# The end of a graph-network kernel: the last rows before the next-to-last batch's closing stages, and the last batch interleaved with it

## The chip, the cores and the metric

The kernel runs on one core of one Trainium2 chip, in one launch. The metric is the device time in microseconds, the median of 3 runs. The core has five engines that run side by side and meet at semaphores: TensorE (PE in the profile; PEld is its weight load), VectorE (DVE), ScalarE (ACT), GpSimd (POOL) and SyncE (SP, which here only issues transfers).

## What is computed

One message-passing layer over 6250 nodes of 128 features and 100000 edges, sorted by destination, with a residual sum and two layer norms. Cut to what matters:

```python
msg_in = concat([x[src], x[dst], edge_attr])           # (100000, 128 + 128 + 4)
h = silu(msg_in @ mW1 + mb1)
messages = h @ mW2 + mb2
aggregated = segment_sum(messages, dst, num_segments=6250)
u = silu(concat([x, aggregated]) @ uW1 + ub1)
updated = u @ uW2 + ub2
y = layer_norm(x + updated, ln_g, ln_b)
out = layernorm(x + y)
```

All of it is float32.

## The kernel before, in words

**Tables.** First, x @ mW1's source part is written to DRAM as `tab_a`, and the destination part as `tab_b`. x is also kept transposed in SBUF (`xT`).

**Edges.** The 100000 edges are cut into 98 groups (`NG`) of 1024, each of 8 tiles of 128 edges; the last group, 97, has 6 tiles. For each group, GpSimd gathers the source rows of `tab_a` by an indirect DMA for each tile (`fetch`, L277) into a tile `ga`, of which a ring of 6 exists. TensorE makes the destination part (`products`, L623) in a PSUM tile `pre` (two buffers). VectorE adds the two (`hidden`, L640), ScalarE takes the Silu (L641) into `h`. TensorE then multiplies h by a one-hot matrix of destinations (`sums`, L652, 16 instructions for 8 tiles), and VectorE adds the result to the running table `acc` and, once in four groups, the degrees to `deg` (`add`, L665 and L670). One pass of the loop at L680 does one group and issues the gathers of the group two ahead.

**Node batches.** What comes after the sum, for each node, is done in batches of 4 tiles of 128 nodes, in `node_batch` (L466). The next-to-last batch has 3 tiles (from tile 44) and the last one 2 (117 nodes by 2). `node_batch` is a generator: each `next` issues one stage, and `advance` issues one stage of every running batch. A batch starts when the groups that reach its nodes have been added. The stages of an ordinary batch are:

1. load of `xs` (x, L495), copies of its part of acc and deg (L500, L501)
2. matmuls into y: u1x by xT (L510), mb2u by degrees (L511), w2u by sums (L515)
3. Silu into uT (L518)
4. bias and u2 matmuls (L521, L530)
5. y + xs and its moments (L532, L483, L484), xs + bias of the norm (L535)
6. square root for the standard deviation (L489)
7. reciprocal, norm into z, moments of z (L539 to L548)
8. square root (L489)
9. reciprocal and shift on VectorE (L552, L554)
10. scale and shift on ScalarE (Identity, L560)
11. write to the output (L564)

The last batch (`final=True`) reads `acc` and `deg` in place, makes two versions of x by two VectorE adds at its second stage (L507, L508), and has one more `yield` between L511 and L515. Its tiles come from the ring of `ga`, and its y is a buffer of `pre`. Before its load stands a VectorE memset (L494), as its tile isn't filled to 128 partitions.

**Order.** The order of all instructions on the engines is the order in which the code issues them (a manual schedule). The next-to-last batch starts in the pass of group 95 with four stages; the pass of group 96 issues four more, ending with stage 8. After the loop come, in this order: the last batch's load; a one-element Silu (`primed`, L748) that brings ScalarE's Silu table back; add(96); the last batch's second stage; the last group's rows in two pieces (`piece`, L731: add L732, Silu L733, sums L652); add(97); two stages of the last batch; and then the rest of both batches, stage by stage in turn.

Of the kernel before, what the change touches and what calls it, by code (L numbers as in the profile page):

```python
# [8 lines left out]
F32 = mybir.dt.float32  # L9
# [3 lines left out]
OP = mybir.AluOpType  # L13
# [5 lines left out]
P = 128  # L19
# [5 lines left out]
def kernel(  # L25
# [40 lines left out]
    nc = tc.nc  # L66
    N, H = x.shape
# [4 lines left out]
    G = 8  # L72
    GE = G * P
    NG = -(-E // GE)
# [11 lines left out]
    BT = 4  # L86
# [16 lines left out]
    batches = [(i0, n, (i0 + n) * P * E // (N * GE) + 1) for i0, n in groups(NT - LAST, BT)]  # L103
# [315 lines left out]
    def rows_ps():  # L419
        return ps.tile([P, G, P], F32, name="pre")  # L420
# [45 lines left out]
    def node_batch(i0, n, work, new, y, final=False):  # L466

        cols = slice(i0 * P, (i0 + n) * P)
        m = (min((i0 + n) * P, N) - i0 * P) // n
        assert m * n == min((i0 + n) * P, N) - i0 * P  # L470

        def rows_of(t):

            return t[i0 * P : i0 * P + m * n].rearrange("(p j) f -> p j f", j=n)

        def flat(t):
            return t[:, :n].rearrange("p i f -> p (i f)")

        def moments(v):
            mv = work.tile([P, BT, 2], F32, name="mv", bufs=2)  # L480
            for i in range(n):
                st = work.tile([P, 6], F32, name="st", bufs=2)
                nc.vector.bn_stats(st, v[:, i, :])  # L483
                nc.vector.bn_aggr(mv[:, i, :], st)  # L484
            return mv

        def std(mv):
            r = work.tile([P, BT], F32, name="r", bufs=2)
            nc.scalar.activation(r[:, :n], mv[:, :n, 1], AF.Sqrt, bias=eps)  # L489
            return r  # L490

        xs = new("xs")
        if m < P:
            nc.vector.memset(xs[m // 32 * 32 :, :n], 0.0)  # L494
        nc.sync.dma_start(xs[:m, :n], rows_of(x))  # L495
        sums, counts = acc[:, cols], deg[:, cols]
        if not final:

            acc_b, deg_b = new("acc_b"), new("deg_b", DR)
            nc.scalar.copy(flat(acc_b), sums)  # L500
            nc.scalar.copy(flat(deg_b), counts)  # L501
            sums, counts = flat(acc_b), flat(deg_b)
        yield
        xb = xs
        if final:
            xb = new("xb")
            nc.vector.tensor_add(xb[:, :n], xs[:, :n], b_b[:, None, :].to_broadcast([P, n, H]))  # L507
            nc.vector.tensor_add(xs[:, :n], xs[:, :n], ub2_b[:, None, :].to_broadcast([P, n, H]))  # L508
        y = y()
        nc.tensor.matmul(flat(y), u1x, xT[:, cols], start=True, stop=False)  # L510
        nc.tensor.matmul(flat(y), mb2u, counts, start=False, stop=False)  # L511
        if final:

            yield
        nc.tensor.matmul(flat(y), w2u, sums, start=False, stop=True)  # L515
        yield
        uT = new("uT")
        nc.scalar.activation(flat(uT), flat(y), AF.Silu, bias=ub1_col)  # L518
        yield
        if not final:  # L520
            nc.tensor.matmul(  # L521
                y[:, :n],
                ones[0:1, :],
                ub2_row[:, None, :].to_broadcast([1, n, H]),
                start=True,
                stop=False,
            )
        by_p = flat(uT).rearrange("k (p j) -> k p j", j=n)
        for i in range(n):
            nc.tensor.matmul(y[:, i, :], by_p[:, :, i], u2, start=final, stop=final or i == n - 1)  # L530
        yield
        nc.vector.tensor_add(y[:, :n], y[:, :n], xs[:, :n])  # L532
        mv = moments(y)
        if not final:
            nc.vector.tensor_add(xs[:, :n], xs[:, :n], b_b[:, None, :].to_broadcast([P, n, H]))  # L535
        yield
        r = std(mv)
        yield
        nc.vector.reciprocal(r[:, :n], r[:, :n])  # L539
        z = new("z")  # L540
        for i in range(n):
            nc.vector.scalar_tensor_tensor(
                y[:, i, :], y[:, i, :], mv[:, i, 0:1], g_b, op0=OP.subtract, op1=OP.mult
            )
            nc.vector.scalar_tensor_tensor(
                z[:, i, :], y[:, i, :], r[:, i : i + 1], xb[:, i, :], op0=OP.mult, op1=OP.add
            )
        mz = moments(z)  # L548
        yield
        rz = std(mz)  # L550
        yield
        nc.vector.reciprocal(rz[:, :n], rz[:, :n])  # L552
        shift = work.tile([P, BT], F32, name="shift", bufs=2)
        nc.vector.scalar_tensor_tensor(  # L554
            shift[:, :n], mz[:, :n, 0], -1.0, rz[:, :n], op0=OP.mult, op1=OP.mult
        )
        yield
        o = z
        for i in range(n):
            nc.scalar.activation(  # L560
                o[:, i, :], z[:, i, :], AF.Identity, bias=shift[:, i : i + 1], scale=rz[:, i : i + 1]
            )
        yield
        (nc.scalar if final else nc.sync).dma_start(rows_of(out), o[:m, :n])  # L564

    def node_tiles(pool, y):
        return pool, lambda name, p=P: pool.tile([p, BT, H], F32, name=name), y
# [1 line left out]
    def advance(running):  # L569

        for b in list(running):
            if next(b, running) is running:
                running.remove(b)
# [70 lines left out]
    def degrees(g):  # L644
        pt = ps.tile([P, 2 * W], F32, name="pt")
        if g % DQ == 0:
            nc.tensor.transpose(pt[:DR, W:], deg_q[g // DQ % 2], ident[:W, :W])  # L647
        return pt
# [14 lines left out]
    def add(g, pt):  # L663
        at = acc[:, bass.ds(bases[g], W)]
        nc.vector.tensor_add(at, at, pt[:, :W])  # L665
        if g % DQ == 0:
            for k in range(min(DQ, NG - g)):
                row = slice(32 * k, 32 * k + 1)
                at = deg[row, bass.ds(bases[g + k], W)]
                nc.vector.tensor_add(at, at, pt[row, W:])  # L670
# [9 lines left out]
    for g in range(NG):  # L680
        if g == 1:
            load_weights()
        if g == 2:
            running.append(destination_checks(node_y()))
        if g == 8:
            running.append(fuse_weights())
        for c in range(1, NC):
            if g == max(1, c * EC // GE - 10):
                attributes(c)
            if g == max(1, c * EC // GE - 10) + 1:  # L690
                attribute_rows(c)
        if g + LEAD < NG:
            load(g + LEAD)
        last = g >= NG - 1
        if not last:
            h[g] = hidden(g)
        if g + 2 < NG:
            pre[g + 2] = products(g + 2)
        if g + MADE < NG:
            node_matrix(g + MADE)  # L700
        if g + 1 < NG:
            oh[g + 1] = edge_matrix(g + 1)
        if g - 2 in pt:
            add(g - 2, pt.pop(g - 2))
        if last:
            break
        pt[g] = by_nodes(g, h.pop(g), oh.pop(g))
        if CLOSE <= g + 2 < NG:
            fetch(g + 2, begun[g + 2], summing[g])
        elif g == 0:  # L710
            fetch(7, ended[1], begun[2])
        elif g == 1:
            fetch(8, begun[3], summing[1])
        elif g % 2:
            fetch(g // 2 + 8, ended[g + 1], begun[g + 2] if g == CLOSE - 3 else ended[g + 2])
        if g >= NG - 3:
            add(g - 1, pt.pop(g - 1))
        for i0, n, first in batches[:-1]:
            if g == (first if first >= NG - 3 else first + 1):
                running.append(node_batch(i0, n, *node_tiles(nodes, node_y)))  # L720
        for _ in range(4 if g >= NG - 3 else 2 if g >= NG - 6 else 1):
            advance(running)

    g = NG - 1
    n = tiles_of(g)
    ga, pg, oh_g, h_g = rows.pop(g), pre.pop(g), oh.pop(g), hbuf[g % NH]
    s = work.tile([P, G, H], F32, name="s")
    primed = consts.tile([1, 1], F32, name="primed")
    before = running.pop()

    def piece(lo, hi):  # L731
        nc.vector.tensor_add(s[:, lo:hi], ga[:, lo:hi], pg[:, lo:hi])  # L732
        nc.scalar.activation(h_g[:, lo:hi], s[:, lo:hi], AF.Silu)  # L733
        sums(g, pt[g], h_g, oh_g, lo, hi)

    final = node_batch(
        *batches[-1][:2],
        nodes,

        lambda name, p=P: gath.tile([P, G, H], F32, name="ga")[:p, :BT],  # L740
        lambda: rows_ps()[:, :BT],
        final=True,
    )
    while running:
        advance(running)
    next(final)

    nc.scalar.activation(primed, ones[0:1, 0:1], AF.Silu)  # L748
    add(g - 1, pt.pop(g - 1))
    pt[g] = degrees(g)  # L750
    next(final)
    piece(0, n - 2)
    piece(n - 2, n)
    add(g, pt.pop(g))
    for _ in range(2):
        next(final)
    running = [before, final]
    while running:
        advance(running)
# [157 lines left out]
```

## Time and profile before

| | us |
|---|---|
| median of 3 runs | 1012.25 (1011.08 to 1012.56) |
| the profiled execution | 1179.78 |
| its span, first to last instruction | 1177.7 |
| the last group's first row add (L732) starts at | 1159.17 |
| the last write (L564, from ScalarE's queue) is issued at | 1172.79 |

The profiled execution is longer than the runs that are timed. Times in views of the profile are counted from the span's start. The granted TensorE clock is 0.668 of full speed in the mean of the span. A chain of waits is read backwards from the last instruction: at each step it goes to what released the instruction, or to the one before it on the same engine, and so names what ended last.

### The profile page before, as it was taken

How to read it: one execution, taken by the hardware profiler on the slowest of the kernel's cores; microseconds unless marked ns; L12 is line 12 of the kernel's file. 1: busy time of each engine (PE TensorE's matmuls, PEld its weight loads, DVE VectorE, ACT ScalarE, POOL GpSimd, SP SyncE). 2: the span in 40 equal slices, each digit the busy share in tenths (PEclk: the TensorE clock that was granted, in tenths of full speed). 3: DMA queues.
4: the chain of work that ended last, by engine and by line, in shares of the span. 5: the costliest groups of instructions: out<-in, count | busy, mean ns of one | idle time of the engine just before them, and what ended most of it. 6: DMA issues, size and time to landing. Idle time of an engine off the chain costs nothing.

```text
span 1177.7 us, 11313 instructions
## 1 busy us (share of the span) xinstructions
PE 747.7 (63%) x3645; PEld 675.3 (57%) x3645; DVE 486.4 (41%) x1017; ACT 238.9 (20%) x297; POOL 743.2 (63%) x790
## 2 busy tenths in 40 slices
PE   5776896656756666567647666656566565656654
PEld 4575786555655656465646565555565464656533
DVE  4461654433532523532533353342343252353344
ACT  2211121220321311120221121121132131122132
POOL 6646666665666666666666666666666666656660
PEclk9877877676565666567566667666666667667665
DMA  8762232222222221222222213221222222212110
GB/s 198 203 156 71 75 85 65 67 82 61 74 66 73 67 72 52 79 72 73 55 72 76 58 57 81 65 81 56 71 74 66 71 74 63 65 55 69 47 59 20
DMA packets 70076, 89.01 MB, mean 76 GB/s; under 512 B 20703, under 2 KB 51694, under 8 KB 70010
## 3 DMA queue, kind: packets, MB, share of 16 engines
q0 software_dynamic: 25024, 51.30, 15.8%
q1 hardware_dynamic: 40408, 35.03, 10.3%
q10 hardware_dynamic: 4578, 1.89, 0.7%
q8 instruction: 31, 0.51, 0.2%
q14 instruction: 35, 0.29, 0.1%
HBM read 76.78 MB, written 11.38 MB: 75 GB/s over the span
## 4 chain that ended last, share of the span: by engine, by line
PE 35%; issue 32%; POOL 20%; DVE 2%; DMA 1%; another core or an unknown queue 1%; ACT 1%; DVEq 0%; POOLq 0%; SPq 0%; ACTq 0%
POOL ga L277 20%; PE pre L623 17%; PE pt L652 14%; PE pre L626 1%; PE y L530 1%; DMA ga<-tab_a,src_i 1%; PE y L521 1%; PE y L510 1%; PE y L511 0%; PE y L515 0%; DVE s L640 0%; DVE st L483 0%; DVE oh L609 0%; PE pt L647 0%
## 5 line engine op out<-in xcount | busy, mean ns | idle before, releaser
L277 POOL DMA_INDIRECT ga<-tab_a,src_i x742 | 703.7, 948 | 384.2 <-issue 187.1
L623 PE MATMUL pre<-mv,st 100*128 100x128 f32 x1564 | 345.1, 396 | 229.5 <-issue 199.5
L623 PEld LDWEIGHTS pre<-mv,st 100*128 100x128 f32 x1564 | 315.2, 301 | 248.4 <-issue 224.3
L652 PE MATMUL pt<-oh,h 128*128 128x96 f32 x1564 | 293.7, 348 | 147.6 <-issue 143.8
L652 PEld LDWEIGHTS pt<-oh,h 128*128 128x128 f32 x1564 | 279.9, 266 | 165.8 <-issue 162.3
L640 DVE TENSOR_TENSOR s<-ga,pre 128x1024 f32<-128x1024 f32 x92 | 112.2, 1220 | 502.6 <-DMA ga<-tab_a,src_i 419.8
L641 ACT ACTIVATE h<-s 128x1024 f32<-128x1024 f32 x92 | 97.1, 1056 | 671.5 <-issue 409.6
L596 DVE TENSOR_SCALAR_CACHE_REDUCE st<-near,p_next 96x1024 f32<-96x1024 uint8 x98 | 124.3, 1270 | 2.9 <-DMA near<-near_d 1.5
L609 DVE TENSOR_TENSOR oh<-w_row,rel 128x768 f32<-128x768 f32 x98 | 93.0, 949 | 42.5 <-remote 42.2
L277 POOL DMA_INDIRECT ga<-in_x_dram,src_i x32 | 30.7, 960 | 16.4 <-issue 8.8
L532 DVE TENSOR_TENSOR y<-y,xs 128x512 f32<-128x512 f32 (+1 forms) x12 | 8.3, 688 | 74.4 <-issue 70.7
L641 ACT ACT_TABLE_LOAD x23 | 29.5, 1283 | 24.2 <-PE pre L626 17.6
L489 ACT ACT_TABLE_LOAD x24 | 30.8, 1283 | 6.1 <-DVE st L483 5.7
L377 PE MATMUL wide<-w,xT 128*128 128x256 f32 x98 | 27.6, 441 | 3.5 <-DVE x_sb L380 3.5
L665 DVE TENSOR_TENSOR acc<-acc,pt 128x96 f32 x98 | 23.7, 242 | 12.5 <-PE pt L652 7.7
L530 PEld LDWEIGHTS y<-u,uT 128*128 128x128 f32 x94 | 22.7, 326 | 10.7 <-issue 10.7
L518 ACT ACTIVATE uT<-y,ub_col 128x512 f32<-128x512 f32 (+1 forms) x12 | 8.1, 678 | 96.5 <-remote 83.6
L377 PEld LDWEIGHTS wide<-w,xT 128*128 128x128 f32 x98 | 21.5, 227 | 8.3 <-DVE x_sb L380 4.3
L530 PE MATMUL y<-u,uT 128*128 128x128 f32 x94 | 25.4, 423 | 0.0
L670 DVE TENSOR_TENSOR deg<-deg,pt 1x96 f32 x98 | 24.4, 249 | 1.0
L626 PE MATMUL pre<-w,ga 128*128 128x128 f32 x80 | 19.4, 326 | 2.7 <-issue 2.6
L521 PE MATMUL y<-ub_row,ones 1*128 1x512 f32 (+1 forms) x24 | 15.5, 729 | 6.9 <-ACT uT L518 6.9
(118 smaller groups left out, 361.7 us busy)
## 6 DMA issues: line engine op xcount, KB each, us to landing
ga<-tab_a,src_i POOLq DMA_INDIRECT x742
near<-near_d SPq DMA_DIRECT2D x24, 384.0 KB
mv<-tab_b SPq DMA_DIRECT2D x98, 48.0 KB
tab_a<-t SPq DMA_DIRECT2D x6, 512.0 KB
tab_b<-x_sb SPq DMA_DIRECT2D x6, 512.0 KB
xs<-in_x_dram SPq DMA_DIRECT2D x11, 256.0 KB
out_dram<-z SPq DMA_DIRECT2D x11, 256.0 KB
st<-ea_d SPq DMA_DIRECT2D x98, 16.0 KB
```

Of the source, the lines that this page charges most:

```text
L277: ins = nc.gpsimd.indirect_dma_start(out=rows[g][:, i, :], out_offset=None, in_=x if g < RAW else tab_a[:, :], in_offset=bass.IndirectOffs ...
L377: ins = nc.tensor.matmul(pm[:, j], xT[:, cols], w1, start=True, stop=True)
L489: nc.scalar.activation(r[:, :n], mv[:, :n, 1], AF.Sqrt, bias=eps)
L521: nc.tensor.matmul(y[:, :n], ones[0:1, :], ub2_row[:, None, :].to_broadcast([1, n, H]), start=True, stop=False,)
L530: nc.tensor.matmul(y[:, i, :], by_p[:, :, i], u2, start=final, stop=final or i == n - 1)
L596: nc.vector.tensor_scalar(stbuf[g % NST][:W], near.pop(g), p_next, 0.0, op0=OP.is_equal, op1=OP.add, accum_out=deg_q[g // DQ % 2][:, g % D ...
L609: nc.vector.tensor_tensor(oh, w_row[:, None, :].to_broadcast([P, G, W]), rel[:, g, :, None].to_broadcast([P, G, W]), op=OP.is_equal,)
L623: ins = nc.tensor.matmul(pre[:, i, :], st[:, i, :], mv[g % NM], start=True, stop=g >= RAW)
L626: ins = nc.tensor.matmul(pre[:, i, :], rows[g][:, i, :], w1[:, 0, :], start=False, stop=True)
L640: nc.vector.tensor_add(s[:, :n], ga[:, :n], ps[:, :n])
L641: nc.scalar.activation(h[:, :n], s[:, :n], AF.Silu)
L652: ins = nc.tensor.matmul(pt[:, :W], h[:, i, :], oh[:, i, :], start=i == 0, stop=i == tiles_of(g) - 1)
```

## The change

It has four parts.

- In the pass of group 95 the last batch is created and its first stage issued (memset and load of x). In the pass of group 96 the next-to-last batch is not advanced at all (it was by four stages), and the last batch's second stage is issued: the two adds of x and the u1x matmul. The extra `yield` stands ahead of the mb2u matmul now, so this moves to the third stage.
- After the loop the last group's rows come first, in two pieces as before, and then add(96).
- Then come the remaining stages of both batches in an order written out by hand: two of the next-to-last batch, the one-element Silu, add(97), and then the two in turn.
- At the end of the last batch, the shift on VectorE and the two Identity passes on ScalarE give way to one subtract-and-multiply on VectorE for each tile (`tensor_scalar`), and the write follows from ScalarE's queue in the same stage.

```diff
@@ node_batch
         nc.tensor.matmul(flat(y), u1x, xT[:, cols], start=True, stop=False)
+        if final:
+
+            yield
         nc.tensor.matmul(flat(y), mb2u, counts, start=False, stop=False)
-        if final:
-
-            yield
         nc.tensor.matmul(flat(y), w2u, sums, start=False, stop=True)
...
         nc.vector.reciprocal(rz[:, :n], rz[:, :n])
+        if final:
+            for i in range(n):
+                nc.vector.tensor_scalar(
+                    z[:, i, :], z[:, i, :], mz[:, i, 0:1], rz[:, i : i + 1],
+                    op0=OP.subtract, op1=OP.mult,
+                )
+            nc.scalar.dma_start(rows_of(out), z[:m, :n])
+            return
...
-        (nc.scalar if final else nc.sync).dma_start(rows_of(out), o[:m, :n])
+        nc.sync.dma_start(rows_of(out), o[:m, :n])
@@ the loop over groups
-        for _ in range(4 if g >= NG - 3 else 2 if g >= NG - 6 else 1):
+        for _ in range(0 if g == NG - 2 else 4 if g == NG - 3 else 2 if g >= NG - 6 else 1):
             advance(running)
+        if g == NG - 3:
+            final = node_batch(
...
+                final=True,
+            )
+            next(final)
+        if g == NG - 2:
+            next(final)
@@ after the loop
-    before = running.pop()
-
-    def piece(lo, hi):
+    (before,) = running
+    pt[g] = degrees(g)
+    for lo, hi in ((0, n - 2), (n - 2, n)):
         nc.vector.tensor_add(s[:, lo:hi], ga[:, lo:hi], pg[:, lo:hi])
         nc.scalar.activation(h_g[:, lo:hi], s[:, lo:hi], AF.Silu)
         sums(g, pt[g], h_g, oh_g, lo, hi)
-
-    final = node_batch(
...
-    while running:
-        advance(running)
+    add(g - 1, pt.pop(g - 1))
+    next(before)
+    next(before)
+
+    nc.scalar.activation(primed, ones[0:1, 0:1], AF.Silu)
+    add(g, pt.pop(g))
     next(final)
-
-    nc.scalar.activation(primed, ones[0:1, 0:1], AF.Silu)
-    add(g - 1, pt.pop(g - 1))
-    pt[g] = degrees(g)
     next(final)
-    piece(0, n - 2)
-    piece(n - 2, n)
-    add(g, pt.pop(g))
-    for _ in range(2):
-        next(final)
+    next(before)
+    next(final)
+    next(before)
+    next(final)
+    next(final)
+    next(before)
+    next(final)
     running = [before, final]
     while running:
         advance(running)
```

More of the change, by code (lines that the diff above doesn't have):

```diff
@@ L510, in node_batch @@
         nc.tensor.matmul(flat(y), u1x, xT[:, cols], start=True, stop=False)
-        nc.tensor.matmul(flat(y), mb2u, counts, start=False, stop=False)
         if final:
             yield
+        nc.tensor.matmul(flat(y), mb2u, counts, start=False, stop=False)
         nc.tensor.matmul(flat(y), w2u, sums, start=False, stop=True)
@@ L720 @@
                 running.append(node_batch(i0, n, *node_tiles(nodes, node_y)))
-        for _ in range(4 if g >= NG - 3 else 2 if g >= NG - 6 else 1):
+        for _ in range(0 if g == NG - 2 else 4 if g == NG - 3 else 2 if g >= NG - 6 else 1):
             advance(running)
+        if g == NG - 3:
+            final = node_batch(
+                *batches[-1][:2],
+                nodes,
+                lambda name, p=P: gath.tile([P, G, H], F32, name="ga")[:p, :BT],
+                lambda: rows_ps()[:, :BT],
+                final=True,
[3 more added lines that the diff above has]
+            next(final)
     g = NG - 1
@@ L734, in piece @@
         sums(g, pt[g], h_g, oh_g, lo, hi)
-    final = node_batch(
[L737 to L743, printed above, removed]
-    while running:
-        advance(running)
+    add(g - 1, pt.pop(g - 1))
[3 more added lines that the diff above has]
+    add(g, pt.pop(g))
     next(final)
-    nc.scalar.activation(primed, ones[0:1, 0:1], AF.Silu)
-    add(g - 1, pt.pop(g - 1))
-    pt[g] = degrees(g)
     next(final)
-    piece(0, n - 2)
-    piece(n - 2, n)
-    add(g, pt.pop(g))
-    for _ in range(2):
-        next(final)
+    next(before)
[5 more added lines that the diff above has]
+    next(final)
     running = [before, final]
```

## The prediction

> **What bounds the kernel now.** I read the page first (busy shares, issues), then the table of waits, then the chain of waits over the last 33 us, then the timeline of the same stretch. The page says that no engine is full, and that GpSimd with its gathers is the most regular of them:
>
> ```profile
> PE 747.7 (63%) x3645; PEld 675.3 (57%) x3645; DVE 486.4 (41%) x1017; ACT 238.9 (20%) x297; POOL 743.2 (63%) x790
> L277 POOL DMA_INDIRECT ga<-tab_a,src_i x742 | 703.7, 948 | 384.2 <-issue 187.1
> ```
>
> and the table of waits says how the gathers wait:
>
> ```profile
> DVE s L640 <- DMA ga<-tab_a,src_i: 419.8, 65, 10.6
> POOL ga L277 <- remote: 141.4, 48, 3.6
> ```
>
> Until the last gather the loop follows GpSimd: a gather starts every 1.25 us, and VectorE waits 419.8 us in all for gathered rows. The 141.4 us of "remote" pauses have no releaser in the program. They are near the 167.5 us by which the profiled execution (1179.78) is longer than the median (1012.25), so I don't take them to be part of the unprofiled time. The change touches nothing before group 95, so all it can move lies after about 1136 us. There the chain of waits reads (start, length, what):
>
> ```profile
> 1149.82 0.58 DVE y L532
> ...
> 1154.46 0.21 DVE st L483
> ...
> 1155.78 0.28 DVE ga L494
> 1156.08 2.08 DMA ga<-in_x_dram
> 1158.16 0.03 issue
> 1158.21 0.04 issue
> 1158.25 0.44 DVE ga L507
> ...
> 1159.17 0.70 DVE s L732
> 1159.89 0.64 ACT h L733
> 1160.53 0.04 issue
> 1160.58 2.89 PE pt L652 x12
> 1163.47 0.03 issue
> 1163.49 0.27 DVE acc L665
> 1163.76 0.04 issue
> 1163.80 1.23 PE pre L515 x2
> 1165.06 0.48 ACT ga L518
> ```
>
> The last rows (group 97) were not late. Their gathers are in the timeline:
>
> ```profile
> 1145.82 0.94 POOL L277 DMA_INDIRECT ga<-tab_a,src_i  x1 [2.46 <-remote]
> 1147.07 0.95 POOL L277 DMA_INDIRECT ga<-tab_a,src_i  x1 [0.30 <-issue]
> 1149.67 3.62 PE L652 MATMUL pt<-oh,h 128*128 128x96 f32 x16
> ```
>
> For group 96 the last gather started at 1136.39 and VectorE could go on at 1138.92, so a gather's rows are usable 2.53 us after its start; those of group 97 were usable at about 1149.6. VectorE reached them at 1159.17, 9.6 us later. In front of them stood the last stages of the batch next to last (L532 at 1149.82 to the last moments at 1155.66: 5.8 us), then a load of x that was issued only at 1156.08 because its memset (L494) stood behind those stages, 2.1 us of waiting for it, and two adds (L507, L508). After 1159.17 the chain is the last batch alone: its sums, a hop to ScalarE, matmuls, and two normalisations to the write at 1172.79. The end of the span, 1177.7, is 4.9 us after that: the write's landing and the closing.
>
> **What the Trainium skill says.** The Trainium skill's "Perfetto Trace Analysis", Per-engine timelines: VectorE, ScalarE and GpSimd take their queues strictly in order. The trace agrees: rows usable at 1149.6 are added at 1159.17. The Trainium skill's "DMA: Bandwidth & Descriptors", Anatomy of one DMA: about 2.0 us fixed for each transfer, stated for GpSimd's path; here, from SP, 2.08 us for the 117 KB of x, so an early issue hides nearly all of it. Its "ScalarE: Activation LUTs", What ACT_TABLE_LOAD costs: 1283 ns plus a drain of 1380 ns. The trace has the 1283 ns and not the drain (loaded at 1147.41 straight behind the 1.04 us Silu), so I use 1.28.
>
> **The change part by part.** Let the common start be the end of the next-to-last batch's u2 matmuls (L530), 1149.72; all that TensorE does before that keeps its place and order.
>
> *Removed:* VectorE's 5.8 us of stages ahead of the last rows, and the 2.1 us load behind them. On SP no queue is overtaken: x of the last batch still follows the write of the batch before (L564, 1138.39). Only its memset now stands behind group 95's work, ending by about 1136.5. SP's semaphore waits for it were over by 1140.5 to 1141.2 in this trace, so x lands at about 1143.3 (+2.08).
>
> *TensorE, the new path.* In its order: sums of group 96 (x16, 3.62) 1149.67 to 1153.3; u1x (L510, 1.11) to 1154.4; sums of group 97 (x12, 2.88) to 1157.3; mb2u (L511, 1.22), which was done in a pause before and now stands behind the sums, to 1158.5; w2u (L515, 1.22) to 1159.75, since the add of group 97 (0.26) is done by 1157.6. Then Silu (0.47 and a hop of 0.05) to 1160.25, u2 (L530 x4, 1.22 and a hop) to 1161.5, and VectorE's y add begins at 1161.6. It began at 1166.92: 5.3 us sooner. The rows of group 97 fit in: first four tiles added after 1147, last two at 1149.6 (+0.41), Silu until about 1150.5, needed at 1154.4. h of group 97 follows h of group 96 in the same table, so no load lies between.
>
> *VectorE beside it.* add(95) at 1145.80, the two x adds (0.43, 0.42) to 1147, the last rows' adds. Then the new wait: add(96) waits for TensorE until 1153.3, and the whole rest of VectorE queues behind it. That add and its two degree rows end at 1154.0 (0.67, as at 1156.08 to 1156.75), the other batch's y and moments at 1156.4 (2.3), add(97) at 1157.6, that batch's z and moments at 1161.2 (3.57, from 1152.09 to 1155.66). Then the last batch's y add, ready at 1161.6: VectorE has only 0.4 us of room, and that is what hides the moved 5.8 us.
>
> *ScalarE.* Three table loads stay three, of 1.28 us. Square root of the next-to-last batch at 1156.4; Silu loaded back to about 1158.0, needed at 1159.75; the next square-root load runs from 1160.2 to 1161.5, and the two roots that use it come at about 1161.5 and 1163. The three Identity passes (1.25) of the next-to-last batch fall beside VectorE's z work of the last batch. Moved, hidden; without this cover an exposed load would cost 1.28.
>
> *The end.* From y to the last moments took 1166.92 to 1171.06, 4.14; the reciprocal and shift of the other batch (0.34) go into the 0.45 us in which VectorE waits for a root. So z's moments end at 1165.75, the root and reciprocal (0.59 before) at 1166.35. Then, instead of shift, hop and two Identity passes (1171.65 to 1172.79, 1.14), two tensor_scalar. The trace has none on 128x128 with two per-partition scalars. Bound below by the 128x2 reciprocal (0.17), above by the scalar_tensor_tensor (0.36, L542). The Trainium skill's "VectorE: DVE Perf Modes", Mode 2×_2P, puts an f32 tensor_scalar within SBUF at two elements a cycle; no run shows it. I take 0.25, near the 0.24 of the 96-column add (L665). With a hop of 0.1: 0.6, that is 0.5 saved (0.3 to 0.7). The write starts at about 1166.95 instead of 1172.79.
>
> *Sum:* 5.3 + 0.5 = 5.8 us, a profiled time of 1174.0 against 1179.78. I carry it to the median nearly whole, 5.5, since one more hop may show among so many turns between two batches: 1012.25 - 5.5 = 1006.7.
>
> **The rivals.** *VectorE becomes the bound, a smaller gain.* The profile grants a clock of 0.50 here; sums of 16 ran in 1.92 us at 1114.10, where the clock was about 0.82. At that speed, and with no pause between the last gathers (rows usable 3.2 us after the common start), VectorE runs 3.25 + 0.35 for rows, 0.75 for add(96), 2.3, 0.3, 3.57 without a gap: y at +10.5. Before, TensorE's part on the chain shrinks by 3.2, from 17.2 to 14.0. Gain 3.5 + 0.4: 1008.3. Against it: the clock reads 0.50 in every stretch from 1149.7 on.
>
> *The last rows are late, no change.* If without the recorder the gathers ended some 9.6 us later against the common start, the 5.8 us and the load of x were hidden already. What remains is mb2u on the path (0.9 beyond the add) less 0.5: 1012.6. Against it: the gathers' pauses are the profile's, and taking out the two in group 97 (1.33 and 2.46) brings the rows sooner, not later.
>
> *The x load blocks VectorE, slower.* The two adds of x now stand ahead of the last rows and of all else on VectorE. If x lands at time Y, y follows 8.76 later (1158.16 to 1166.92), plus 0.9 for mb2u, less 0.5 at the end: slower from Y = 1157.8 on, us for us. At Y = 1160, 1014.5. For it: SP waits for several semaphores before this load, among them a gather's. Against it: even a wait for the last gather (1149.6) lets x land at 1151.7, and the sums could still start at 1154.4.
>
> **How the numbers follow.** Forecast 0.62; VectorE-bound 0.25; rows late 0.08; x blocks 0.05. A measurement of this kernel can tell about 0.2%, 2 us, from no change. The first two lie beyond that almost whole: faster 0.86, same 0.09, slower 0.05. The range goes up to 1009.3, past the VectorE-bound case with the dear tensor_scalar and a table load partly exposed, and down to 1004.9, where the sums of group 96 run at the fast clock while the end keeps the slow one (1.7 us less).
>
> **What would show it.** Right: x lands before 1145; the last rows are added (L732) before 1151; TensorE goes from sums of 96 through u1x to sums of 97 with no gap over 0.5 us; the y add of the last batch stands about 12 us after the u2 matmuls of the other batch, where it was 17.2; two tensor_scalar of about 0.25 end it. Wrong: L507 waiting for x past the last gather; sums of 97 waiting for Silu; VectorE still in the other batch's z work when u2 of the last batch is done by more than 1 us; a table load next to the last Silu.

## The result, and the profile after

| | us |
|---|---|
| median before, 5 runs | 1012.25 (1011.08 to 1012.62) |
| median of the changed kernel, 5 runs | 1007.39 (1006.90 to 1007.52) |
| ratio | 0.9953, 95% interval 0.9938 to 0.9967 |
| predicted | 1006.7, range 1004.9 to 1009.3 |
| profiled execution after: time, span | 1007.52, 1005.4 |

The kernel became 4.9 us faster; 5.5 were forecast. One thing has to be known for every number below: on some chips all runs of the kernel before, timed or profiled, take about 1170 us and the profiles show pauses of about 3.4 us before gathers, on others it takes about 1012 us and the profiles taken there (all of the changed kernel or of variants of it) show none, so a run is compared only with the kernel before on the same chip.

The first profile of the kernel before was of the paused kind and the profile after is not. So whole spans can't be set against each other, but stretches inside the end can. The changed kernel's waits, from the table of waits (engine, line, released by: us in all, times, longest):

```profile
ACT h L649 <- DVE s L648: 649.1, 90, 11.6
DVE s L648 <- DMA ga<-tab_a,src_i: 459.5, 88, 9.7
```

VectorE waits for gathered rows 88 times, and GpSimd has no "remote" wait in this table any more. Next, the timeline of the changed kernel around the last rows (start, length, engine, line, operation, tiles; in brackets the idle time before it and what ended that):

```profile
981.24 1.31 PE L530 MATMUL y<-u,uT 128*128 128x128 f32 x6
981.72 0.42 DVE L507 TENSOR_TENSOR ga<-ga,b_b 128x256 f32<-128x256 f32 x1
...
982.48 1.95 PE L660 MATMUL pt<-oh,h 128*128 128x96 f32 x16
...
984.17 0.94 POOL L277 DMA_INDIRECT ga<-tab_a,src_i  x1 [0.30 <-issue]
...
984.35 0.69 DVE L752 TENSOR_TENSOR s<-ga,pre 128x512 f32<-128x512 f32 x1 [1.74 <-DMA ga<-tab_a,src_i]
...
985.81 1.13 PE L660 MATMUL pt<-oh,h 128*128 128x96 f32 x8 [0.92 <-ACT h L753]
987.68 0.42 DVE L752 TENSOR_TENSOR s<-ga,pre 128x256 f32<-128x256 f32 x1 [2.65 <-DMA ga<-tab_a,src_i]
988.02 0.25 DVE L673 TENSOR_TENSOR acc<-acc,pt 128x96 f32 x1
...
988.61 1.17 PE L660 MATMUL pt<-oh,h 128*128 128x96 f32 x4 [1.67 <-ACT h L753]
...
991.29 1.22 PE L515 MATMUL pre<-acc,w2u 128*128 128x256 f32 x2 [0.60 <-DVE acc L673]
...
993.07 1.22 PE L530 MATMUL pre<-u,ga 128*128 128x128 f32 x4 [0.56 <-ACT ga L518]
...
994.63 0.41 DVE L532 TENSOR_TENSOR pre<-pre,ga 128x256 f32<-128x256 f32 x1
```

The adds of x (L507) start without a wait. Sums of group 96 (L660 x16) are done at 984.43, and then TensorE stands still twice, 0.92 and 1.67 us, because VectorE itself waits for rows, 1.74 and 2.65 us. The last rows set the pace here. Later the w2u matmuls (L515) wait 0.60 us for VectorE's add of group 97, and the last batch's y add (L532) starts 0.34 us after the u2 matmuls (L530) are done at 994.29, without a wait. From the last rows' add to that y add the chain of waits of the changed kernel (start, length, what) is VectorE alone:

```profile
984.17 3.42 DMA ga<-tab_a,src_i
...
988.09 0.11 DVE acc L673
988.20 0.22 DVE deg L678
...
988.71 0.58 DVE y L532
...
990.54 0.48 DVE xs L535
...
991.15 0.17 DVE r L539
...
994.80 1.26 ACT L489
996.05 0.04 issue
996.09 0.30 ACT r L489
```

Before the change the chain from the load of x on held two Silus and three groups of matmuls (sums, w2u, u2). From the last gather on no matmul is left in it. From the add of group 96 (988.02) to the last batch's y add (994.63) VectorE works 6.61 us and waits for no other engine; then a ScalarE table load (L489 at 994.80) is on the chain for once.

### The profile page after: what moved, and what is told of

Read it like the earlier page. It is cut to its first block, busy times and chain, and to the rows that moved or that the text cites. A ratio compares the mean times of both kernels' runs of the same rounds, so it can differ in the third digit from the quotient of the medians.

```text
span 1005.4 us, 11309 instructions
## 1 busy us (share of the span) xinstructions
PE 682.9 (68%) x3645; PEld 627.6 (62%) x3645; DVE 487.0 (48%) x1018; ACT 238.9 (24%) x295; POOL 740.0 (74%) x790
## 5 line engine op out<-in xcount | busy, mean ns | idle before, releaser
L631 PE MATMUL pre<-mv,st 100*128 100x128 f32 x1564 | 328.6, 390 | 282.1 <-DVE s L648 235.6
L631 PEld LDWEIGHTS pre<-mv,st 100*128 100x128 f32 x1564 | 300.5, 293 | 304.4 <-DVE s L648 255.5
L660 PE MATMUL pt<-oh,h 128*128 128x96 f32 x1564 | 254.0, 332 | 7.2 <-DVE deg L678 3.9
L660 PEld LDWEIGHTS pt<-oh,h 128*128 128x128 f32 x1564 | 252.9, 253 | 9.4 <-ACT acc_b L500 3.3
L530 PEld LDWEIGHTS y<-u,uT 128*128 128x128 f32 x94 | 22.5, 323 | 8.9 <-issue 8.9
L530 PE MATMUL y<-u,uT 128*128 128x128 f32 x94 | 25.2, 415 | 0.0
L377 PE MATMUL wide<-w,xT 128*128 128x256 f32 x98 | 23.1, 391 | 0.2 <-DVE rel L200 0.2
L484 DVE BATCH_NORM_AGGREGATE mv<-st 128x2 f32<-128x6 f32 x98 | 17.8, 182 | 3.4
L568 ACT ACTIVATE z<-z,shift,r 128x128 f32<-128x128 f32 x47 | 19.2, 479 | 0.3 <-DVE shift L562 0.3
L545 DVE SCALAR_TENSOR_TENSOR z<-y,r,xs 128x128 f32<-128x128 f32 x47 | 16.5, 351 | 1.7
L542 DVE SCALAR_TENSOR_TENSOR y<-y,mv,g_b 128x128 f32<-128x128 f32 x47 | 16.5, 351 | 1.3
```

The lines of the kernel that those rows point to most:

```text
L377: ins = nc.tensor.matmul(pm[:, j], xT[:, cols], w1, start=True, stop=True)
L631: ins = nc.tensor.matmul(pre[:, i, :], st[:, i, :], mv[g % NM], start=True, stop=g >= RAW)
L660: ins = nc.tensor.matmul(pt[:, :W], h[:, i, :], oh[:, i, :], start=i == 0, stop=i == tiles_of(g) - 1)
```

## The experiments

Theory A is the forecast's: TensorE's queue from the next-to-last batch's u2 matmuls sets the end. Theory B came from the profile above: VectorE's queue sets it, from the add of group 96 or the last rows on, whichever comes later. Stretches that I compare: from the next-to-last batch's u2 end to the last write's issue ("u2 to write"), from the add of group 96 to the last batch's y add ("add to y"), and from there to the write.

### Runs on chips with pauses

**The kernel before, again.** No edit.

> The kernel before, profiled once more. If the pauses without a releaser in its first profile (48 before gathers, 141 us) belong to that recording, they are gone here, the span is near 1010 us, and group 97's rows are usable about 3 to 5 us after the next-to-last batch's u2 matmuls, as they are in the changed kernel (5.1 us). The chain of waits still goes through that batch's z, the load of x and the last rows' add. If the pauses belong to the kernel, they are there again.

One profiled execution: 1172.64 us, and the pauses are there again:

```profile
POOL ga L277 <- remote: 136.9, 48, 3.4
```

All timed runs on that chip took 1167 to 1172 us, as long as the profiled one, so the recording doesn't account for the pauses. u2 to write is 23.0 us, as in the first profile (23.1), though the last gather started 7.6 us before the u2 end here and 2.7 there. In these two profiles the stretch doesn't depend on when the last rows land. Whether this holds without pauses wasn't seen: no profile of the kernel before without them was taken.

**Early load alone.**

```diff
+        if g == NG - 3:
+            final = node_batch(
...
+            next(final)
 ...
-    final = node_batch(...)      # after the loop
...
-    next(final)
```

> The kernel before with one part of the change: the last batch's memset and load of x in the pass of group 95; its second stage and all else where they were. Theory that the load's wait is a part of the gain: about 2.2 us faster than before (1010.0), and the adds of x follow the next-to-last batch's moments without a wait. Rival, that the order of the rows does everything and the load would be hidden: no change from before.

Ratio 0.9985, interval 0.9978 to 0.9992: 1168.15 us, 1.7 us faster than before (1169.81) in the medians. u2 to write fell from 23.0 to 21.1 us. The timeline has the adds of x without a wait behind the degree rows, where the kernel before waited for x:

```profile
1147.87 0.50 DVE L670 TENSOR_TENSOR deg<-deg,pt 1x96 f32 x2
1148.16 1.28 ACT L746 ACT_TABLE_LOAD   x1
1148.40 0.43 DVE L507 TENSOR_TENSOR ga<-ga,b_b 128x256 f32<-128x256 f32 x1
```

In the old order the load was a real part of the loss.

**The new order with the late load.** The last batch is created after the loop, its first two stages ahead of the last rows.

> The changed kernel with the early load undone: the last batch is created after the loop, and its first two stages are issued there, directly ahead of the last rows. Theory that VectorE waits for the last rows anyway: the load (about 2.1 us) ends before the last rows land, so within 0.4 us of the changed kernel (1007.4 to 1007.8). Rival, that the early load is 2 us of the gain in this order too: 1009.5.

Ratio 0.9953 (0.9937 to 0.9969). The changed kernel itself was not run on this chip, so the profile decides. VectorE waits for x, and it costs nothing:

```profile
1139.25 0.43 DVE L507 TENSOR_TENSOR ga<-ga,b_b 128x256 f32<-128x256 f32 x1 [2.45 <-DMA ga<-in_x_dram]
...
1140.05 1.21 DVE L750 TENSOR_TENSOR s<-ga,pre 128x512 f32<-128x512 f32 x2
1140.06 3.62 PE L660 MATMUL pt<-oh,h 128*128 128x96 f32 x16
...
1143.71 0.26 DVE L673 TENSOR_TENSOR acc<-acc,pt 128x96 f32 x1 [2.45 <-PE pt L660]
```

The 2.45 us wait ends at 1139.25; the rows are added at once, and then VectorE waits again, for the sums of group 96. Add to y is 6.63 us. So the two parts of the change are not additive: in this profile the order alone hides the load as well. On a chip without pauses, where VectorE doesn't wait for these sums, this wasn't tried.

**The old end of the last batch.** The `if final:` block with the two tensor_scalar is taken out, so that shift, Identity passes and write are as before.

> The changed kernel with the end of the last batch as before: shift on VectorE, hop, two Identity passes on ScalarE, in place of two tensor_scalar. Both theories: 0.5 us slower (1007.9), since 1.14 us stood there before and 0.63 us stands there now. Nothing hides it. If it is not slower, the write's landing and not its start sets the end.

Ratio 0.9940 (0.9926 to 0.9953); times of one kernel on such a chip differ by up to 5 us and don't resolve half a microsecond. From the last batch's y add to the write: 6.19 us here, 5.72 to 5.74 in the other runs that keep the changed kernel's end and its late table load. The new end is worth 0.46 us, where 0.5 were expected.

**TensorE work doubled.**

```diff
+        if final:
+            nc.tensor.matmul(flat(y), u1x, xT[:, cols], start=True, stop=True)
         nc.tensor.matmul(flat(y), u1x, xT[:, cols], start=True, stop=False)
```

> The changed kernel with the last batch's u1x matmul issued twice (the second overwrites the first), which puts 0.6 to 1.1 us more of TensorE work between the sums of group 96 and those of group 97. Theory of the forecast, that TensorE's queue without gaps sets the end: 0.6 to 1.1 us slower (1008.0 to 1008.5). Theory that the last rows and then VectorE set it: no change, as TensorE waits for the rows there.

1162.16 us, ratio 0.9925 (0.9905 to 0.9944); the changed kernel itself was not run on this chip, and its other variants there lie at 0.9920 to 0.9940. The profile says more:

```profile
1142.46 0.26 DVE L675 TENSOR_TENSOR acc<-acc,pt 128x96 f32 x1 [2.07 <-PE pt L662]
...
1142.72 0.59 PE L512 MATMUL pre<-xT,u1x 128*128 128x256 f32 x2
...
1143.15 1.47 PE L662 MATMUL pt<-oh,h 128*128 128x96 f32 x12
...
1145.43 0.25 DVE L675 TENSOR_TENSOR acc<-acc,pt 128x96 f32 x1
```

Add to y is 6.62 us, with 0.6 us more of matmuls ahead of the sums of group 97: as long as in the changed kernel. This speaks against theory A for that stretch. The reason is not the one that was expected, though: TensorE doesn't wait for rows there. The sums of group 97 are done at 1144.62, and VectorE comes to add them 0.81 us later. Where the stretch begins is TensorE's doing on this chip, as VectorE waits 2.07 us for the sums of group 96.

**The add of group 96 between the pieces, and the other batch's y ahead of the rows.**

```diff
+    next(before)                              # second run only
     pt[g] = degrees(g)
     for lo, hi in ((0, n - 2), (n - 2, n)):
...
+        if lo == 0:
+            add(g - 1, pt.pop(g - 1))
-    add(g - 1, pt.pop(g - 1))
-    next(before)                              # second run only
```

> The changed kernel with the add of group 96 (one acc row block and two degree rows, 0.7 us of VectorE) between the two pieces of the last rows, where VectorE waits for the last two tiles. VectorE theory: this work leaves the chain, 0.6 to 0.7 us faster (1006.7). TensorE theory: no change.

> As the run that puts the add of group 96 between the pieces, and the next-to-last batch's y and moments (2.3 us of VectorE) ahead of the last rows as well, into VectorE's wait for them. VectorE theory: 2.3 us and 0.7 us leave VectorE's chain, until TensorE's path (sums of 97, w2u, Silu, u2) or the square-root and Silu table loads take over, so 1.0 to 1.6 us faster than the changed kernel (1005.8 to 1006.4). TensorE theory: no change or slower, as rows are added later.

Ratios 0.9940 (0.9920 to 0.9960) and 0.9920 (0.9902 to 0.9938): inconclusive in time. In the profile of the first, a pause had held the sums of group 96 back to 1141.2. The last two tiles' add then had to wait behind that of group 96, with no wait for their rows left. In the second, add(97) waited 2.25 us for the sums of group 97, so TensorE set the pace there. Neither shows a gain that the times can tell, and neither tests the theory where the rows come last.

**xs + b made early.**

```diff
+        if i0 == batches[-2][0]:
+            xb = new("xb")
+            nc.vector.tensor_add(xb[:, :n], xs[:, :n], b_b[:, None, :].to_broadcast([P, n, H]))
...
-        if not final:
+        if xb is xs:
```

> The changed kernel with the next-to-last batch's xs + b (0.5 us of VectorE after its moments) made at its second stage into a tile of its own, in the pass of group 95. VectorE theory: 0.4 to 0.5 us faster (1006.9). TensorE theory: no change.

Ratio 0.9930 (0.9911 to 0.9949). Add to y fell from 6.62 to 6.48 us only, against 0.4 to 0.5 expected. That add had stood in the time in which ScalarE takes the square root; without it VectorE waits for it:

```profile
1146.02 0.18 DVE L542 RECIPROCAL r<-r 128x3 f32<-128x3 f32 x1 [0.16 <-ACT r L489]
```

A miss for theory B in its simple form: taking work off the engine that sets the end gains only as much as that work wasn't covering a wait.

### Runs on one chip without pauses

The kernel before took 1012.64 us here (11 runs, 1011.8 to 1013.44).

**The changed kernel, again.**

> The changed kernel once more, as the control of this call, beside the kernel before on the same chip. Both theories: VectorE takes 6.6 us without a gap from the add of group 96 to the y add of the last batch, and 2.1 to 2.2 us from there to that batch's first norm pass, where the kernel before takes 1.8.

1008.10 us, ratio 0.9957 (0.9943 to 0.9970).

```profile
982.99 3.73 PE L660 MATMUL pt<-oh,h 128*128 128x96 f32 x16 [0.98 <-ACT h L649]
...
988.55 0.42 DVE L752 TENSOR_TENSOR s<-ga,pre 128x256 f32<-128x256 f32 x1 [2.48 <-DMA ga<-tab_a,src_i]
988.88 0.25 DVE L673 TENSOR_TENSOR acc<-acc,pt 128x96 f32 x1
...
995.50 0.41 DVE L532 TENSOR_TENSOR pre<-pre,ga 128x256 f32<-128x256 f32 x1
```

The sums of group 96 took 3.73 us here and 1.95 in the first profile of the same kernel; the profiles grant a TensorE clock of 0.50 and of 1.00 in these stretches. Even so they are done at 986.72, and VectorE still waits for rows until 988.55. Add to y is 6.62 us, against 6.61: matmuls of nearly twice the length changed nothing in it. This speaks against theory A without pauses too. From the y add to the first norm pass 2.15 us, where the kernel before has 1.82 (1166.92 to 1168.74).

**VectorE work added.**

```diff
     add(g - 1, pt.pop(g - 1))
+    more = work.tile([P, G, H], F32, name="s")
+    for i in range(0, 6, 3):
+        nc.vector.tensor_add(more[:, i : i + 3], b_b[...], ub2_b[...])
     next(before)
```

> The changed kernel with two more adds on VectorE (128x384 each, of constants into a spare tile) directly behind the add of group 96. Theory that VectorE's queue from that add on sets the end: the stretch from the add to the y add of the last batch grows by their whole length, 0.9 to 1.1 us, and so does the time. Theory that TensorE's path sets it: VectorE's work lies beside TensorE's, 0 to 0.4 us.

1009.90 us (1009.18 to 1011.92), ratio 0.9969 (0.9958 to 0.9981), 1.8 us above the changed kernel on this chip in the median (1007.99 to 1009.27). The two adds took 1.03 us:

```profile
991.41 0.25 DVE L673 TENSOR_TENSOR acc<-acc,pt 128x96 f32 x1
...
992.10 1.03 DVE L758 TENSOR_TENSOR s<-b_b,ub_b 128x384 f32<-128x384 f32 x2
...
999.09 0.41 DVE L532 TENSOR_TENSOR pre<-pre,ga 128x256 f32<-128x256 f32 x1
```

Add to y is 7.68 us (991.41 to 999.09), 1.06 more than the 6.62 of the run above: all of the added work. The last gather to the write grew by 1.02 us. The remaining 0.8 us of the median isn't explained. The profiled execution was the slowest of the seven (1011.92), and in it the last gather itself started 2.6 us later than in the run above. The direction and the stretch are theory B's.

**The square-root table early.**

```diff
     next(final)
     next(final)
+    nc.scalar.activation(primed, ones[0:1, 0:1], AF.Sqrt)
     next(before)
```

> The changed kernel with a one-element square root on ScalarE directly behind the last batch's Silu, so that the table for square roots is loaded beside VectorE's work and not when the next-to-last batch's moments are there. Theory that the load is exposed (it starts with those moments, and the last batch's root waits behind it): from the last batch's y add to its first norm pass 1.8 us in place of 2.15, 0.3 to 0.4 us faster. Rival, that VectorE's reciprocals fill that wait anyway: no change.

1007.74 us (1006.24 to 1008.85), 0.36 below the changed kernel, within the spread of both. The stretch is clear: from the y add to the first norm pass 1.80 us, and 5.38 in place of 5.73 to the write. The load now lies beside VectorE's work on the other batch's z:

```profile
993.05 1.28 ACT L763 ACT_TABLE_LOAD   x1
...
994.66 0.41 DVE L532 TENSOR_TENSOR pre<-pre,ga 128x256 f32<-128x256 f32 x1
...
996.46 0.34 DVE L542 SCALAR_TENSOR_TENSOR pre<-pre,mv,g_b 128x128 f32<-128x128 f32 x1
```

**All three moves.** The other batch's y ahead of the rows, the add of group 96 between the pieces, and the early table.

> The next-to-last batch's y and moments ahead of the last rows, the add of group 96 between their two pieces, and the early square-root table together. VectorE theory, on a chip without pauses in the gathers: 1.0 us of VectorE work leaves the chain before TensorE and ScalarE take over, and 0.3 us at the end: 1.3 us faster than the changed kernel. Where a pause holds back the sums of group 96, only the 0.3 us and some tenths remain. TensorE theory: 0.3 us at most.

1007.25 us (1006.45 to 1007.90), ratio 0.9947 (0.9933 to 0.9960). Its five runs all lie below the changed kernel's five (1007.99 to 1009.27). From the last rows' add to the write: 11.39 us (987.83 to 999.22) against 12.68 (988.55 to 1001.23), 1.29 us less, where 1.3 were expected. In the median 0.85 us of it showed. Against the early table alone the times overlap, but the stretch is 0.95 us shorter (12.34 there, 987.70 to 1000.04). This is the test of theory B by moving work where the rows come last:

```profile
982.61 0.56 DVE L532 TENSOR_TENSOR y<-y,xs 128x384 f32<-128x384 f32 x1
...
985.84 0.25 DVE L673 TENSOR_TENSOR acc<-acc,pt 128x96 f32 x1 [0.28 <-PE pt L660]
...
987.83 0.42 DVE L753 TENSOR_TENSOR s<-ga,pre 128x256 f32<-128x256 f32 x1 [1.33 <-DMA ga<-tab_a,src_i]
...
989.48 0.26 DVE L673 TENSOR_TENSOR acc<-acc,pt 128x96 f32 x1 [1.23 <-PE pt L660]
...
990.34 0.18 DVE L539 RECIPROCAL r<-r 128x3 f32<-128x3 f32 x1 [0.61 <-ACT r L489]
```

The moved 3 us fill most of the wait for the rows. Afterwards VectorE waits 1.23 us for the sums of the last two tiles and 0.61 us for a root, whose table ScalarE loads only after the last rows' Silu (988.72 to 990.00). So what follows the last rows on other engines is the bound now, and about 2 of the 3 us are lost to it.

## Why the prediction was right, and where not

**The sign, the place and nearly the size** were right: 4.9 and 4.5 us in the two sets of runs without pauses, 5.5 forecast. VectorE's stages and the load of x left the way of the last rows. The load in itself was worth 1.7 us in the old order, on a chip with pauses.

**The likeliest case named the wrong engine, and the nearness of its number is in part luck.** The step "TensorE, the new path" fails: in both profiles of the changed kernel without pauses, VectorE waits for rows and then works without a wait until y. More of TensorE's work cost nothing in that stretch (u1x twice on a chip with pauses, slower sums on one without), more of VectorE's cost its full length. One of the forecast's own signs of being right, no gap over 0.5 us in TensorE from the sums of group 96 to those of group 97, is missed (0.92 and 1.67), and the sums of group 97 wait for Silu, a sign of being wrong. It is the first rival, VectorE as the bound (1008.3 forecast, chance 0.25), that happened, together with rows later than it took them. The measured 1007.39 lies between the two.

The forecast put the last batch's y add 11.9 us after the other batch's u2 end. It came at 12.1 in the first profile and at 13.6 (981.93 to 995.50) in the second: the near match of the first comes from rows that were later and sums that were shorter than forecast. How the gain divides over these terms stays open, as no profile shows the end of the kernel before without pauses.

What the runs show of the path:

- *When the last rows are usable.* This term decides. I set 2.53 us from a gather's start to its use, read from group 96 in the paused profile. The last gather of the changed kernel needed 3.51 (984.17 to 987.68). I also put the rows at the u2 end (-0.1 us); without pauses they came 5.1 us after it, and 6.6 in the second profile. The rival's 3.2 us was short as well.
- *The matmuls' speed.* I took the durations of the kernel before's end, where the clock reads 0.50: 3.62 us for the 16 sums, 2.88 for the 12. In the changed kernel the 16 took 1.95 us in one profile and 3.73 in the other. So the figure was a possible one, and the rival's condition of a fast clock wasn't needed: VectorE is the bound at both. (The 0.82 that I gave for the sums at 1114.10 is the mean of 1110 to 1120; the stretch from 1113.5 to 1116.2 reads 0.99.)
- *The root's table.* "The next square-root load runs from 1160.2 to 1161.5", hidden, was wrong: it starts with the other batch's moments (994.80, after 994.71) and ends when the last batch's moments are there too (996.08). So the other batch's reciprocal and shift (0.34 us), which I had put into VectorE's wait for a root, come after that wait, ahead of the last batch's first norm pass. It costs 0.33 us, and the run with the early table got back 0.35.

**VectorE's own sum was near:** 0.67, 2.3, 0.3 and 3.57, together 6.8 us, measured 6.61. "VectorE has only 0.4 us of room" was the line to act on: with so little, the two paths were one forecast, and their chances should have been closer together.

**The end:** tensor_scalar at 0.25 each and a hop of 0.1 for the two were near (0.60 for two and 0.03 to the write); the 0.5 us saved is the 0.46 of the run with the old end. Net of the exposed table load only 0.14 of it is seen: 5.87 us from y to the write before, 5.73 after.

**The pauses.** That they are no "part of the unprofiled time" held for the runs it was said of, but that "the gathers' pauses are the profile's" falls: on two chips the timed runs were as slow as the profiled ones that show them.

**The rivals that fell.** The x load didn't block VectorE in the changed kernel without pauses (L507 follows add(95) at once), and a wait of 2.45 us for it, with the late load and pauses, cost nothing. Rows coming late was half right: they are what VectorE waits for, but 5 to 7 us after the common start, not 9.6.

Open: what causes the pauses, what each part of the change is worth without them, and the 0.8 us by which the run with more VectorE work was slower than its own stretch explains.

## What to carry to other kernels

At the end of a kernel that is paced by gathers, put what needs the last rows first in the queues, and put the independent work not behind the rows but into the wait for them: 3 us moved into that wait were worth about 1 here, because other engines took over as the bound. If the working of a prediction leaves two engines within half a microsecond of each other, forecast with both, and test by adding work to one of them at a time. Where a function needs another table on ScalarE, try a one-element call of it as soon as the last use of the old table is issued; here it shortened the end by 0.35 us. Don't take the length of matmuls from one profile alone: the same 16 took 1.95 and 3.73 us in two profiles of one kernel.

## What the hardware showed that was not expected

- A table load on ScalarE sometimes starts right behind the instruction ahead (988.57, while its root follows only at 990.66) and sometimes only when the root's inputs are there (994.80). The one-element call turned the second kind into the first, worth 0.35 us.
- Two chips ran every execution 16% slower (1170 us against 1012), with 46 to 51 pauses of up to 3.6 us before gathers for which the profiles show no releaser in the program. In the end stretch VectorE, ScalarE and GpSimd come out of a pause at nearly the same time: in the first profile of the kernel before, at 1145.80, 1145.87 and 1145.82.
